# A scan kernel whose partitions hold four states by 32 channels in place of two states by 64

## The chip, the cores and the metric

The kernel runs on one core of one Trainium2 chip. The metric is the device time of one execution in microseconds, lower is better. The kernel before took 8292.5 us (median of 3 runs, 8291.23 to 8294.32). A core has four compute engines that run side by side, each with its own instruction queue: TensorE (PE) multiplies matrices, VectorE (DVE), ScalarE (ACT) and GpSimd (POOL) work elementwise, and SyncE (SP) issues the transfers. Data lies in SBUF, 128 partitions of plain memory, or in PSUM, eight banks that PE accumulates into. Transfers are moved by 16 DMA engines.

## The reference

The input is x of 8 x 512 x 48 x 48 in float32, so 8 samples of 512 channels and 2304 places. Layer 0 is a group norm and causal linear attention with a residual. Layer 1 is a group norm and then, for each of four blocks of 128 channels in turn, a Mamba block with 256 inner channels and 16 states. Its core is a recurrence in time, for every inner channel d and state n:

```
delta = softplus(dt @ Wdt.T + bdt);  A = -exp(A_log)
h[d,n] = exp(delta[d] * A[d,n]) * h[d,n] + (delta[d] * xs[d]) * B[n]      # one step in time
y[d]   = sum over n of h[d,n] * C[n]
y = (y + xs * D) * silu(z);  output = y @ Wo.T
```

B and C are 16 rows in time that all channels share; delta and dx = delta * xs are 256 rows in time that all states share.

## The kernel before

Time is cut into 6 chunks of LC = 384 places. A job is one chunk of one block of one sample; there are 8 x 4 x 6 = 192 jobs, taken from two streams in turn (even and odd samples). A job has 256 x 16 = 4096 recurrences, which fill 128 partitions 32 times, so it has 32 scans. They stand in 8 slots of 4 scans. In each slot the partitions hold 2 states (i) by 64 channels, and the four scans are two state pairs (j) by two groups of channels (g).

For each job the program prepares its operands (`prepare`, L697). ACT makes delta and POOL makes dx, both with 128 channels on the partitions. Two transfers write them to DRAM scratch (`spread`, L787), and others read them back in the layout of the scans: `dr` (delta, L802) and `dxr` (dx, L806), one tile for each half h of the 256 channels, each in two transfers of 64 partitions (`pairs`, L798). The rows of B and C go to DRAM scratch as well (`scr`, L763) and come back as four tiles each (`rows`, L810), a row being copied to 64 partitions by a source whose first dimension has step 0. All these transfers are issued by SP, in the order of the program.

A slot then works as follows.

- `decay` (L890): ACT writes exp(scale * dr) to a PSUM bank, once for each scan.
- `inputs` (L854): ACT copies the first 256 places of dxr to a PSUM bank as `dxp`, twice for each job.
- `product` (L881): DVE forms B * dx for the first 256 places, from B in SBUF and dxp in PSUM. `last_product` (L866): POOL forms the last 128 places, from SBUF.
- `scan` (L902): DVE runs the recurrence, 384 places for each scan.
- `weigh` (L915): POOL multiplies the four scans by C.
- `gather` (L930): PE adds the states of each channel into the bank `yp`, by a matrix of ones and zeros with 64 columns (`pair_sum`, L94), once for each scan.

Everything else (the convolution and gates of the Mamba block, the attention of later samples) is woven in between these slots. The order on every queue is written when the program is built: a slot is two halves, and a task says at which half its next step may be put (`yield first - 7, 0` means seven halves before its job's first slot; `Task`, L989, `beside`, L1069). In steady state a slot of job n carries the scans of job n, the preparation of job n + 1 and a piece of attention. `slot` (L1150) asks for `last_product` of slot k + 2 in the middle of slot k, and for `product` of slot k + 1 at the start of slot k.

Of the kernel before, what the change touches and what calls it, by code (L numbers as in the profile page):

```python
# [9 lines left out]
F32 = mybir.dt.float32  # L10
# [7 lines left out]
P = 128  # L18
T = 128
LC = 384  # L20
NG = 2
# [8 lines left out]
C_ID, C_MASK, C_GRP, C_ALL, C_TRI, C_SEL, C_END = 0, 128, 256, 384, 512, 640, 642  # L30


def constants():

    c = np.zeros((P, C_END), np.float32)
    p = np.arange(P)
    c[:, C_ID : C_ID + P] = p[:, None] == p[None, :]
    c[:, C_MASK : C_MASK + P] = p[:, None] <= p[None, :]
    c[:, C_GRP : C_GRP + P] = np.where(p[:, None] // 16 == p[None, :] // 16, 1.0 / 16.0, 0.0)
    same = p[:, None] % 64 == p[None, :] % 64  # L40
    c[:, C_ALL : C_ALL + P] = same
    c[:, C_TRI : C_TRI + P] = same & (p[:, None] // 64 <= p[None, :] // 64)

    for e in range(2):
        c[e * 64 : e * 64 + 64, C_SEL + e] = 1.0
    return c
# [3 lines left out]
def attention_then_mamba_kernel(  # L50
# [33 lines left out]
    k_all = cst[:, C_ALL : C_ALL + P]  # L84
# [8 lines left out]

    pair_sum = k_all[:, 0:64]  # L94
# [20 lines left out]
    w_a = scales[:, :, 596:628].rearrange("p s (h d) -> p s h d", h=4)  # L115
# [15 lines left out]
    drs = [cpool.tile([P, 2, 1 + LC], F32, name=f"dr_{i}") for i in range(2)]  # L131
# [392 lines left out]
    class Stream:  # L524
# [37 lines left out]
        def move_on(self):  # L562

            if self.b is not None and self.s < 3:
                self.s += 1
                self.fresh = False
            else:
                self.b, self.s = self.samples.pop(0), 0
                self.fresh = True
            self.ready = 0  # L570
            self.block += 1
            self.n = f"{self.b}_{self.s}"
            self.state = small.tile(
                [P, 2, NS // 2, 2], F32, tag=f"state{self.z}", name=f"state_{self.n}", bufs=1
            )
            self.fsum = small.tile([P, NC], F32, tag=f"fsum{self.z}", name=f"fsum_{self.n}", bufs=1)
            self.fm = dpool.tile([P, L], F32, tag="fm", name=f"fm_{self.n}")
            self.w = self.coming
# [111 lines left out]
    class Job:  # L690
# [6 lines left out]
        def prepare(self):  # L697
# [89 lines left out]
            def spread(what, of):  # L787
                to = dpool.tile([256, LC], F32, tag="dscr", name=f"{what}_{n}", bufs=6)
                nc.sync.dma_start(out=to.rearrange("(h p) l -> p h l", h=2), in_=of)
                return to.rearrange("(h g d) l -> h d g l", h=2, g=2)  # L790
# [5 lines left out]
            src = scr.rearrange("(q i m f) l -> q m i (f l)", q=4, m=2, i=2)  # L796

            def pairs(t, rows):  # L798
                for i in range(2):
                    nc.sync.dma_start(out=t[i * 64 : i * 64 + 64], in_=rows)  # L800

            def steps(h):  # L802
                self.dr[h] = drs[h]
                pairs(self.dr[h][:, :, 1 : 1 + LC], dsrc[h])

            def scaled(h):  # L806
                self.dxr[h] = mpool.tile([P, 2, LC], F32, tag="dxr", name=f"dxr_{n}_{h}")
                pairs(self.dxr[h], xsrc[h])

            def rows(m, q):  # L810
                t = mpool.tile([P, NG, LC], F32, tag="BC"[m], name=f"{'BC'[m]}_{n}_{q}", bufs=4)
                for i in range(2):
                    nc.sync.dma_start(
                        out=t[i * 64 : i * 64 + 64].rearrange("p j l -> p (j l)"),
                        in_=src[q, m, i].partition_broadcast(64),
                    )
                (self.B, self.C)[m][q] = t
# [7 lines left out]
            spreading.clear()  # L825
            yield first - 7, 0
            flush()
            steps(0)
            scaled(0)
            yield first - 6, 0  # L830
            rows(0, 0)
            yield first - 5, 0
            rows(0, 1)
            self.prepared = True
            yield first - 3, 0
            rows(0, 2)
            yield first - 2, 0
            rows(1, 0)
            yield first - 1, 0
            rows(0, 3)  # L840
            yield first, 0
            rows(1, 1)
            yield first + 1, 0
            scaled(1)
            yield first + 2, 0
            rows(1, 2)
            yield first + 3, 0
            steps(1)
            yield first + 4, 0
            rows(1, 3)  # L850
# [3 lines left out]
        def inputs(self, h):  # L854

            self.dxp = psx.tile([P, 2, LC - TAIL], F32, tag="dxp", name=f"dxp_{self.n}_{h}")
            nc.scalar.copy(self.dxp, self.dxr[h][:, :, 0 : LC - TAIL])  # L857
# [8 lines left out]
        def last_product(self, s):  # L866

            shape, cols = [P, NG, 2, TAIL], slice(LC - TAIL, LC)
            u = mpool.tile([P, NG, 2, 1 + LC], F32, tag="u", name=f"u_{self.n}_{s}", bufs=5)
            if self.c:  # L870
                h, q = s // 4, s % 4 * NG
                nc.scalar.copy(u[:, :, :, 0], self.state[:, h, q : q + NG, :])
            nc.gpsimd.tensor_tensor(  # L873
                u[:, :, :, 1 + LC - TAIL :],
                self.B[s % 4][:, :, cols].unsqueeze(2).to_broadcast(shape),
                self.dxr[s // 4][:, :, cols].unsqueeze(1).to_broadcast(shape),
                ALU.mult,
            )
            return u

        def product(self, s, u):  # L881

            shape, cols = [P, NG, 2, LC - TAIL], slice(0, LC - TAIL)
            nc.vector.tensor_mul(  # L884
                u[:, :, :, 1 : 1 + LC - TAIL],
                self.B[s % 4][:, :, cols].unsqueeze(2).to_broadcast(shape),
                self.dxp.unsqueeze(1).to_broadcast(shape),
            )

        def decay(self, s, i):  # L890
            h, q, j, g = s // 4, s % 4 * NG, i // 2, i % 2
# [6 lines left out]
                scale=w_a[:, self.w[1], 2 * h + g, q + j : q + j + 1],  # L898
# [3 lines left out]
        def scan(self, s, i, u, dA):  # L902
            j, g = i // 2, i % 2
            cols = slice(0 if self.c else 1, 1 + LC)
            nc.vector.tensor_tensor_scan(  # L905
                u[:, j, g, cols],
                dA[:, cols],
                u[:, j, g, cols],
# [6 lines left out]
        def weigh(self, s, u):  # L915

            nc.gpsimd.tensor_tensor(  # L917
                u[:, :, :, 0:LC],
                u[:, :, :, 1:],
                self.C[s % 4].unsqueeze(2).to_broadcast([P, NG, 2, LC]),  # L920
# [3 lines left out]
        def keep(self, s, u):  # L924

            h, q = s // 4, s % 4 * NG
            if self.c + 1 < NC:
                nc.scalar.copy(self.state[:, h, q : q + NG, :], u[:, :, :, LC])

        def gather(self, s, u):  # L930
            for j in range(NG):
                for g in range(2):
                    nc.tensor.matmul(  # L933
                        self.yp[g * 64 : g * 64 + 64, 0:LC],
                        pair_sum,
                        u[:, j, g, 0:LC],
                        start=False,
                        stop=(s % 4 == 3 and j == NG - 1),
                        skip_group_check=True,
                    )  # L940
# [209 lines left out]
    def slot(k):  # L1150
# [12 lines left out]
        for i in range(4):  # L1163
# [8 lines left out]
            if i == 1:  # L1172
# [5 lines left out]
                if s == 2:  # L1178
                    job.inputs(1)
# [125 lines left out]
```

## Time and profile before

The profiled execution took 8294.55 us by its own time, and its span, from the first to the last instruction, is 8292.4 us.

| engine | busy us | share of the span |
|---|---|---|
| DVE | 7952.3 | 96% |
| POOL | 7759.7 | 94% |
| PE | 7748.5 | 93% |
| ACT | 6911.0 | 83% |
| 16 DMA engines, mean of their packets' time | | 72% for SP's queue |

The first scan starts at 192.9 us and the last one ends at 8270.4 us. The 192 jobs therefore take 42.07 us each, a slot 5.26 us and a half 2.63 us. Busy time alone does not say what limits the kernel: one engine that is late in each job sets the pace of all, since every queue is served in order.

### The profile page before, as it was taken

The numbers are of one execution on the slowest core, as the hardware profiler recorded it, in microseconds if no ns is written. First come the engines' busy times: TensorE is split into PE (matmuls) and PEld (weight loads), VectorE is DVE, ScalarE is ACT, GpSimd is POOL, SyncE is SP. The second block draws the span as 40 slices with busy tenths as digits, with TensorE's granted clock in tenths as the row PEclk, the third lists the DMA queues.
The fourth block names the chain that finished last, engine by engine and source line by source line (L and its number), as shares of the span: only waits on it lengthen the run. The fifth ranks groups of instructions, "written<-read, shape, count | busy, mean of one in ns | idle before, by whom it ended". The sixth has DMA issues, their size and how long they took to land. (4 is left out here: it accounts for less than half of the span.)

```text
span 8292.4 us, 128570 instructions
## 1 busy us (share of the span) xinstructions
PE 7748.5 (93%) x38850; PEld 3744.1 (45%) x38850; DVE 7952.3 (96%) x10534; ACT 6911.0 (83%) x14630; POOL 7759.7 (94%) x4235
## 2 busy tenths in 40 slices
PE   8999999998999999999999999999999999999975
PEld 4444444444444444444444444444444444444432
DVE  3999999999999999999999999999999999999998
ACT  3888888887888888888888888888888888888876
POOL 2999999999999999999999999999999999999998
PEclk9999999999999999999999999999999999999987
DMA  6667777766777777777777777777777777777665
GB/s 202 190 190 204 210 206 209 208 193 197 208 204 201 201 208 209 204 205 196 201 207 201 197 205 209 208 208 193 202 200 207 201 201 197 201 200 196 191 169 145
DMA packets 974440, 1654.65 MB, mean 200 GB/s; under 512 B 119337, under 2 KB 768169, under 8 KB 973618
## 3 DMA queue, kind: packets, MB, share of 16 engines
q1 hardware_dynamic: 973746, 1646.43, 72.2%
q8 instruction: 309, 5.06, 0.3%
q14 instruction: 385, 3.15, 0.1%
HBM read 1318.28 MB, written 327.68 MB: 198 GB/s over the span
## 5 line engine op out<-in xcount | busy, mean ns | idle before, releaser
L905 DVE TENSOR_TENSOR_SCAN u<-bank,u 128x385 f32<-128x385 f32 (+1 forms) x6144 | 5439.5, 935 | 132.0 <-ACT bank L894 129.5
L917 POOL TENSOR_TENSOR u<-u,C 128x1536 f32<-128x1536 f32 x1536 | 4901.4, 3191 | 344.6 <-DVE u L905 147.3
L894 ACT ACTIVATE bank<-dr,scales 128x385 f32<-128x385 f32 (+1 forms) x6144 | 3411.6, 578 | 673.8 <-DVE u L905 639.4
L933 PE MATMUL yp<-u,cst 128*64 128x384 f32 x12288 | 2371.8, 507 | 236.2 <-ACT yp L862 160.3
L873 POOL TENSOR_TENSOR u<-B,dxr 128x512 f32<-128x512 f32 x1536 | 1977.2, 1287 | 17.3 <-DMA B<-scr 15.7
L884 DVE TENSOR_TENSOR u<-B,dxp 128x1024 f32<-128x1024 f32 x1536 | 1831.7, 1193 | 8.2 <-ACT dxp L857 8.2
L302 PE MATMUL bank<-xn,wq 128*128 128x384 f32 x4608 | 1659.1, 502 | 90.9 <-POOL xn L326 47.8
L933 PEld LDWEIGHTS yp<-u,cst 128*64 128x64 f32 x12288 | 776.5, 138 | 1412.3 <-issue 997.1
L302 PEld LDWEIGHTS bank<-xn,wq 128*128 128x128 f32 x4608 | 833.2, 191 | 838.4 <-DVE u L905 124.3
L709 PE MATMUL bank<-xi,wk 128*128 128x384 f32 x3072 | 1103.5, 502 | 9.5 <-POOL xi L683 6.3
L709 PEld LDWEIGHTS bank<-xi,wk 128*128 128x128 f32 x3072 | 556.2, 191 | 553.3 <-DVE u L905 94.0
L314 ACT ACTIVATE ex<-bank,bqkv_sb 128x384 f32<-128x384 f32 x384 | 220.3, 574 | 416.2 <-PE bank L302 416.1
L894 ACT ACT_TABLE_LOAD x382 | 490.1, 1283 | 6.7
L822 POOL TENSOR_TENSOR dx<-delta,xs 128x384 f32<-128x384 f32 x384 | 387.4, 1009 | 22.2 <-ACT delta L780 22.2
L951 PE MATMUL bank<-yz,scales 128*128 128x384 f32 x768 | 305.4, 514 | 38.4 <-DVE yz L945 30.6
L769 PE MATMUL bank<-dbc,steps_w 9*128 9x384 f32 x768 | 305.5, 517 | 3.4 <-ACT dbc L761 2.4
L720 PE MATMUL bank<-xi,scales 128*128 128x384 f32 x768 | 290.0, 492 | 2.6 <-ACT xs L745 2.1
L756 PE MATMUL bank<-xs,scales 128*40 128x384 f32 x768 | 279.5, 486 | 0.0
L857 ACT COPY dxp<-dxr 128x512 f32<-128x512 f32 x384 | 227.2, 592 | 37.0 <-DMA dxr<-xscr 19.2
L500 PE MATMUL bank<-sm,v 128*64 128x128 f32 x2304 | 253.0, 298 | 0.0
L745 ACT ACT_TABLE_LOAD x192 | 246.3, 1283 | 4.9 <-PE bank L709 1.5
L780 ACT ACT_TABLE_LOAD x192 | 246.3, 1283 | 4.0 <-issue 0.6
(118 smaller groups left out, 7907.2 us busy)
## 6 DMA issues: line engine op xcount, KB each, us to landing
B<-scr SPq DMA_DIRECT2D x1536, 192.0 KB, 4.6
C<-scr SPq DMA_DIRECT2D x1536, 192.0 KB, 5.2
xn<-xn SPq DMA_DIRECT2D x192, 768.0 KB, 7.1
dr<-dscr SPq DMA_DIRECT2D x768, 192.0 KB, 3.8
dxr<-xscr SPq DMA_DIRECT2D x768, 192.0 KB, 4.8
dscr<-delta SPq DMA_DIRECT2D x192, 384.0 KB, 6.9
xscr<-dx SPq DMA_DIRECT2D x192, 384.0 KB, 2.4
xn<-in_x SPq DMA_DIRECT2D x48, 768.0 KB, 6.6
```

The source lines that it names most:

```text
L302: nc.tensor.matmul(ps, wqs[m // NC][:, kt, j * P : (j + 1) * P], xn[:, kt, :], start=(kt == 0), stop=(kt == 3),)
L709: nc.tensor.matmul(xc, wk[:, k, h * P : (h + 1) * P], xi[:, c0 + k : c0 + k + LC], start=(k == 0), stop=(k == 3),)
L720: nc.tensor.matmul(zp, w_gate[:, s, h * P : (h + 1) * P], xi[:, c0 + 3 : c0 + 3 + LC], start=True, stop=True,)
L769: nc.tensor.matmul(vp, steps_w[32:41, s, h * P : (h + 1) * P], dbc[32:41, :], start=True, stop=True)
L822: nc.gpsimd.tensor_tensor(dx[:, h, :], delta[:, h, :], xs[:, h, :], ALU.mult)
L873: nc.gpsimd.tensor_tensor(u[:, :, :, 1 + LC - TAIL :], self.B[s % 4][:, :, cols].unsqueeze(2).to_broadcast(shape), self.dxr[s // 4][:, :, ...
L884: nc.vector.tensor_mul(u[:, :, :, 1 : 1 + LC - TAIL], self.B[s % 4][:, :, cols].unsqueeze(2).to_broadcast(shape), self.dxp.unsqueeze(1).to ...
L894: nc.scalar.activation(dA[:, cols], self.dr[h][:, g, cols], AF.Exp, scale=w_a[:, self.w[1], 2 * h + g, q + j : q + j + 1],)
L905: nc.vector.tensor_tensor_scan(u[:, j, g, cols], dA[:, cols], u[:, j, g, cols], 0.0, ALU.mult, ALU.add,)
L917: nc.gpsimd.tensor_tensor(u[:, :, :, 0:LC], u[:, :, :, 1:], self.C[s % 4].unsqueeze(2).to_broadcast([P, NG, 2, LC]), ALU.mult,)
L933: nc.tensor.matmul(self.yp[g * 64 : g * 64 + 64, 0:LC], pair_sum, u[:, j, g, 0:LC], start=False, stop=(s % 4 == 3 and j == NG - 1), skip_g ...
L951: nc.tensor.matmul(self.xm[:, 0:LC], w_out[:, self.w[1], h, :], self.yz[:, h, :], start=(h == 0), stop=(h == 1),)
```

## The change

The partitions hold 4 states (i) by 32 channels. In each slot the four scans are four groups of 32 channels (g) of one half, at one group of states (q). The states of a channel are now added by four products of 32 columns. A dxr or dr tile has four groups per partition where it had two, and B and C have two tiles per job where they had four. In `inputs`, B is copied to PSUM (`Bp`) and dxr is read from SBUF, with four copies for each job. The transfers change in form, number and order:

```
             def spread(what, of):
                 to = dpool.tile([256, LC], F32, tag="dscr", ...)
-                nc.sync.dma_start(out=to.rearrange("(h p) l -> p h l", h=2), in_=of)
-                return to.rearrange("(h g d) l -> h d g l", h=2, g=2)
+                for h in range(2):
+                    nc.sync.dma_start(
+                        out=to.rearrange("(h c g) l -> h g c l", h=2, g=NGR)[h],
+                        in_=of[:, h, :],
+                    )
+                return to.rearrange("(h c g) l -> h c g l", h=2, g=NGR)
             def steps(h):
-                pairs(self.dr[h][:, :, 1 : 1 + LC], dsrc[h])
+                for i in range(NI):
+                    nc.sync.dma_start(
+                        out=self.dr[h][i * 32 : i * 32 + 32, :, 1 : 1 + LC], in_=dsrc[h]
+                    )
             def scaled(h):
-                self.dxr[h] = mpool.tile([P, 2, LC], F32, tag="dxr", ...)
-                pairs(self.dxr[h], xsrc[h])
+                self.dxr[h] = mpool.tile([P, NGR, LC], F32, tag="dxr", ...)
+                rows = xsrc[h].rearrange("c g l -> c (g l)")
+                nc.sync.dma_start(
+                    out=self.dxr[h].rearrange("p g l -> p (g l)"),
+                    in_=rows.unsqueeze(0).to_broadcast([NI, 32, NGR * LC]),
+                )
-            def rows(m, q):
-                t = mpool.tile([P, NG, LC], F32, tag="BC"[m], ..., bufs=4)
-                for i in range(2):
-                    nc.sync.dma_start(
-                        out=t[i * 64 : i * 64 + 64].rearrange("p j l -> p (j l)"),
-                        in_=src[q, m, i].partition_broadcast(64),
-                    )
+            def rows(m, half):
+                t = mpool.tile([P, 2, LC], F32, tag="BC"[m], ..., bufs=2)
+                src = scr.rearrange("(m q i f) l -> m q i (f l)", m=2, q=2, i=NI)[m, half]
+                nc.sync.dma_start(
+                    out=t.rearrange("p f l -> p (f l)"),
+                    in_=src.unsqueeze(1).to_broadcast([NI, 32, 2 * LC]),
+                )
```

The transfers stand at these halves relative to the job's first slot. Before: dr 0 and dxr 0 at -7, B at -6, -5, -3, -1, C at -2, 0, 2, 4, dxr 1 at 1, dr 1 at 3. After: B 0 at -8, dr 0 and dxr 0 at -7, B 1 at -4, C 0 at -2, dxr 1 at 0, dr 1 at 1, C 1 at 3.

```
-        def inputs(self, h):
-            self.dxp = psx.tile([P, 2, LC - TAIL], F32, tag="dxp", ...)
-            nc.scalar.copy(self.dxp, self.dxr[h][:, :, 0 : LC - TAIL])
+        def inputs(self, pair):
+            self.Bp = psx.tile([P, 2, LC - TAIL], F32, tag="Bp", ...)
+            nc.scalar.copy(self.Bp, self.B[pair % 2][:, :, 0 : LC - TAIL])
         def product(self, s, u):
-                self.B[s % 4][:, :, cols].unsqueeze(2).to_broadcast(shape),
-                self.dxp.unsqueeze(1).to_broadcast(shape),
+                self.Bp[:, s % 2, :].unsqueeze(1).to_broadcast(shape),
+                self.dxr[s // NQ][:, :, cols],
         def gather(self, s, u):
-            for j in range(NG):
-                for g in range(2):
-                    nc.tensor.matmul(self.yp[g * 64 : g * 64 + 64, 0:LC], pair_sum, u[:, j, g, 0:LC], ...)
+            for g in range(NGR):
+                nc.tensor.matmul(self.yp[g * 32 : g * 32 + 32, 0:LC], state_sum, u[:, g, 0:LC], ...)
         # in slot(), in the middle of a slot
-                if s == 2:
-                    job.inputs(1)
+                if s in (0, 2, 4):
+                    job.inputs(s // 2 + 1)
```

`decay`, `scan`, `weigh`, `keep` and `last_product` change their indices alone: the same number of instructions on as many elements. The order of instructions on PE, DVE and POOL stays as it was.

## The prediction

> **What bounds the kernel now.** I read the page's busy shares first, then the groups by line, then the waits, then the transfers.
>
> ```profile
> PE 7748.5 (93%) x38850; PEld 3744.1 (45%) x38850; DVE 7952.3 (96%) x10534; ACT 6911.0 (83%) x14630; POOL 7759.7 (94%) x4235
> ...
> DMA packets 974440, 1654.65 MB, mean 200 GB/s; under 512 B 119337, under 2 KB 768169, under 8 KB 973618
> ...
> q1 hardware_dynamic: 973746, 1646.43, 72.2%
> ...
> L905 DVE TENSOR_TENSOR_SCAN u<-bank,u 128x385 f32<-128x385 f32 (+1 forms) x6144 | 5439.5, 935 | 132.0 <-ACT bank L894 129.5
> L917 POOL TENSOR_TENSOR u<-u,C 128x1536 f32<-128x1536 f32 x1536 | 4901.4, 3191 | 344.6 <-DVE u L905 147.3
> ...
> L884 DVE TENSOR_TENSOR u<-B,dxp 128x1024 f32<-128x1024 f32 x1536 | 1831.7, 1193 | 8.2 <-ACT dxp L857 8.2
> ...
> L857 ACT COPY dxp<-dxr 128x512 f32<-128x512 f32 x384 | 227.2, 592 | 37.0 <-DMA dxr<-xscr 19.2
> ```
>
> DVE bounds it: 7952 of 8292 us, of which some 150 lie before the first scan, so it is nearly gapless in the 192 jobs. Scans and products are 7271 us of that. Transfers hardly show: on DVE the longest wait is for ACT's decays (129.5 us). But SP's queue keeps the 16 DMA engines 72% busy on average, so they have a reserve of 1.4 times, and only if the load is spread evenly.
>
> The list of transfers, by line, with KB each and median us from issue to landing:
>
> ```profile
> B<-scr SPq DMA_DIRECT2D x1536, 192.0 KB, 4.6
> C<-scr SPq DMA_DIRECT2D x1536, 192.0 KB, 5.2
> ...
> dr<-dscr SPq DMA_DIRECT2D x768, 192.0 KB, 3.8
> dxr<-xscr SPq DMA_DIRECT2D x768, 192.0 KB, 4.8
> dscr<-delta SPq DMA_DIRECT2D x192, 384.0 KB, 6.9
> xscr<-dx SPq DMA_DIRECT2D x192, 384.0 KB, 2.4
> ...
> steps_w<-in_wdt SPq DMA_DIRECT2D x1, 36.0 KB
> ```
>
> **What the skill says.** (1) The Trainium skill, "DMA: Bandwidth & Descriptors", section "Why a DMA increments its semaphore by 16 and not by 1": a transfer issued by SP runs on k engines, k being the largest number up to 16 that divides the slowest dimension (other than 1) of both access patterns; they are the lowest-numbered k, and each posts one completion. (2) Its "Rules for kernel authors": a leading broadcast of c copies confines the transfer to at most c engines. The trace agrees where it can be tested. The list's counts add up to 7451 transfers; 16 completions each would be 119,216 packets of 4 bytes, and with the 128 rows of 48 bytes of bqkv (its 6 KB) 119,344 packets under 512 B. The page has 119,337, which is 7 fewer: the one transfer with 9 rows, steps_w, posted 9. It is also the one without a landing time. No transfer of before with a first dimension of 4 exists. (3) "SBUF — State Buffer", "Door 1: The DMA port swizzle": partitions p and p + 32 share a port. Packet records agree for reads: isolated ksum stores, 64 partitions, took 115 ns for 1536 bytes in the median, xscr stores on 128 partitions 66 ns. (4) Same page, "Who interferes with whom": DVE with one SBUF input does not contend with GpSimd; product has one SBUF and one PSUM input both ways.
>
> **The change part by part.**
>
> *DVE, POOL, PE:* as many instructions on as many elements, in the same order. Product swaps which input is in PSUM; I keep 1193 ns (bounds: 3% either way on 1832 us, 55 us). POOL's rows keep 1287 and 3191 ns. Gather keeps its 12,288 matmuls at 507 ns, with loads of 32 columns where 64 took 138 ns; PE weight loads overlap. Constants and memsets differ before the first scan by under 1 us.
>
> *ACT:* four copies per job for two. 384 x 592 ns = 227 us more. ACT has 1381 us idle, 639.4 of them waiting for DVE to free a decay's bank; that covers it. Without cover it is 227 us. Behind a late copy wait the decays, and behind them DVE's scans.
>
> *SP:* per job two spreads become four, 8 reads of dr and dxr become 10, 16 of B and C become 4: 18 issues for 26, near 0.6 us each in the timeline, 5 us less. SP is not on the path; worth nothing by itself.
>
> *Bytes:* the same. B and C halve from 604 to 302 MB (3072 x 196,608 bytes before), dr and dxr double from 302 to 604, spreads stay at 151.
>
> *Where the bytes go* is the step that decides. As the instructions carry them, B and C have a source of 4 rows x 32 copies (step 0) on a target of 128 partitions; dxr has 4 copies (step 0) x 32 rows on 128; a spread has a target of 4 x 32 rows from 128. By (1) all run on k = 4 engines, the same four. Only dr (32 on both sides) keeps 16. Per job and engine of the four:
>
> - dxr: 2 x 786,432 bytes / 4 = 393 KB
> - B and C: 4 x 393,216 / 4 = 393 KB
> - spreads: 4 x 196,608 / 4 = 197 KB
> - dr: 8 x 196,608 / 16 = 98 KB
> - everything else: 1646.4 - 604 - 302 - 151 = 589.4 MB, / 192 jobs / 16 = 192 KB
>
> Sum 1273 KB, where it was 1646.43 MB / 192 / 16 = 536 KB. The page's rate of an engine while busy is 1646.43 MB / (0.722 x 16 x 8292.4 us) = 17.2 KB/us. So the four need 1273 / 17.2 = 74.1 us per job, against the job's 42.07 us. They become the bound, and the other twelve idle.
>
> *Sum:* head 192.9 + 192 x 74.1 + tail 22.0 (8292.4 - 8270.4) = 14,440 us, against a span of 8292.4 (own time 8294.55; the median 8292.5 is the same to 0.03%).
>
> *Bounds on the rate.* Fast: the best packets in the records are 65 ns for 1536 bytes, 119 for 3072, 234 for 6144. Then dxr 64 x 234 = 15.0, B and C 128 x 119 = 15.2, spreads 128 x 65 = 8.3, dr 64 x 65 = 4.2, others about 115 x 65 = 7.5, and 1.1 for larger packets and completions: 51.3 us, or 10,065 us in all. Slow: engines 0 and 1 walk partitions 0-31 and 32-63 together, and by (3) share a port at each step, as 2 and 3 do. At the ksum ratio (115/65) on dxr, B, C and spreads: 38.5 x 1.77 + 12.8 = 80.9 us, or 15,760; with rates fully halved, 89.8 us and 17,460. I take the mean rate of before, since its B rows also came in 64-partition transfers and its 3072-byte packets took 191 ns in the mean.
>
> *What is late next.* dxr 0 is issued at half -7 and needed by last_product at half -3, 10.5 us later; 197 KB per engine at 17.2 KB/us take 11.4 us alone, behind B 0's 5.7 and xscr's 5.7. So POOL waits there, with weigh queued behind it; then DVE's product (now a direct reader of dxr), its scans, and the PSUM banks that ACT's decays need. dxr 1 (half 0 to 5) and C 1 (half 3 to 6, 7.9 us) are late too. Every transfer on all 16 engines queues behind the same four, so attention's xr, xn and before arrive late and stall PE.
>
> **The rivals.**
>
> *A. Four engines, but at nearly their best packet rate* (51 to 62 us per job): 10,065 to 12,100, some 10,500 with idle gaps. For it: twelve engines are nearly silent, and half of the 1536-byte packets already take 65 ns. Against: the shared port.
>
> *B. Four engines with ports fully shared:* 15,800 to 17,500, more if the chain xscr, dxr, last_product leaves the engines empty between. For it: the ksum packets. Against: two engines drift apart.
>
> *C, on the other side: the transfers run on 16 engines after all,* because the splitter follows the 128 partitions on the SBUF side. For it: only one transfer of before had fewer than 16, and its 9 rows stood on both sides. Then the load per engine stays 536 KB, with larger dxr packets and 8 issues fewer per job. It frees POOL's 48.2 us before weigh and ACT's 19.2 us of waits for transfers, less what the ACT copies add: about 8270 us, between 8200 and 8340. It decides at k: with k = 8 the load is 755 MB / 192 / 8 + 290 = 782 KB, or 45.5 us, already over 42.07; so only k = 16 escapes.
>
> *D. No engine limit, but the four copies make decays late:* uncovered 227 us, 8520. Against: ACT's 639 us of slack. It goes with C's slow edge.
>
> **How the numbers follow.** The forecast case, 12,000 to 15,800: 0.56. A, below 12,000: 0.18. B above 15,800: 0.09. C with D: 0.17, of which 0.07 faster, 0.05 within 0.2% (about what a measurement of this kernel can tell from no change) and 0.05 slower. Faster 0.07, same 0.05, slower 0.88. The forecast is 14,440. The range from 9,800 to 17,000 holds the first two cases and most of B; C and B's end are left out, some 0.2. The forecast case's own range is 12,000 to 15,800.
>
> **What would show it.** Right: the page's mean DMA share falls to some 40% ((4 x 100% + 12 x 23%) / 16) while time rises; GB/s falls to about 115; packets under 512 B fall to about 71,720, since ten transfers per job post 4 completions (2459 other transfers x 16 - 7 + 192 x (8 x 16 + 10 x 4) + 128), where 16 engines for all would leave 94,760; landing times of dxr and B rise past 10 us; POOL, ACT and DVE wait for DMA dxr, B and C, and DVE's share falls to about 55%. The rows for scans, products and weigh keep 935, 1193 and 3191 ns. Wrong: landings of dxr near 5 us, a DMA share near 70% and a DVE share of 95% would mean that the transfers were spread, and the whole sum falls.

## The result, and the profile after

The kernel after took 11,127.55 us (median of 4 runs, 11,116.35 to 11,155.28) against 8293.41 us for the kernel before (4 runs beside them, 8291.23 to 8298.3): a ratio of 1.342, with a 95% interval of 1.340 to 1.344. The profiled execution took 11,132.0 us, its span 11,130.2.

The forecast was 14,440 us. The direction and the mechanism stand, and the time lies in the wide range from 9,800 to 17,000, but the loss is 2834 us where 6147 were forecast, and the forecast case's own range, 12,000 to 15,800, is missed. This is rival A, four engines at nearly their best packet rate, to which the prediction gave 0.18.

Three words are used below. A packet is one piece that a DMA engine moves, here mostly of 1536, 3072 or 6144 bytes. A completion is the packet of 4 bytes that each engine of a transfer posts at its end. A narrow transfer is one that posts fewer than 16 completions.

The page of the kernel after, with the lines that answer to those shown of before: busy times, transfers, the chain that ended last, and the groups (busy us, mean ns of one, idle time just before them and what ended it):

```profile
PE 8279.8 (74%) x38850; PEld 3844.8 (35%) x38850; DVE 8026.9 (72%) x10534; ACT 7141.4 (64%) x15014; POOL 7764.6 (70%) x4235
...
DMA packets 877653, 1654.25 MB, mean 149 GB/s; under 512 B 71721, under 2 KB 720553, under 8 KB 876850
...
q1 hardware_dynamic: 876978, 1646.19, 49.5%
...
DMA 68%; PE 8%; DVE 8%; POOL 6%; issue 4%; ACT 3%; SPq 2%; POOLq 0%; ACTq 0%; DVEq 0%
...
L900 DVE TENSOR_TENSOR_SCAN u<-bank,u 128x385 f32<-128x385 f32 (+1 forms) x6144 | 5447.1, 938 | 504.1 <-ACT bank L890 423.3
L913 POOL TENSOR_TENSOR u<-u,C 128x1536 f32<-128x1536 f32 x1536 | 4882.7, 3179 | 1129.2 <-DMA C<-scr 740.9
...
L869 POOL TENSOR_TENSOR u<-B,dxr 128x512 f32<-128x512 f32 x1536 | 1958.6, 1275 | 1964.1 <-DMA dxr<-xscr 1502.7
L880 DVE TENSOR_TENSOR u<-Bp,dxr 128x1024 f32<-128x1024 f32 x1536 | 1849.7, 1204 | 1611.2 <-DMA dxr<-xscr 1589.5
...
L853 ACT COPY Bp<-B 128x512 f32<-128x512 f32 x768 | 447.7, 583 | 404.6 <-DMA B<-scr 366.4
...
dxr<-xscr SPq DMA_DIRECT2D x384, 768.0 KB
```

DVE is busy for 75 us more than before and the span is 2838 us longer: the loss is waiting, not work. The scan (935, now 938 ns), the product (1193, 1204) and weigh (3191, 3179) are what they were. DVE waited 8.2 us ahead of its product before and waits 1611.2 now, nearly all for dxr; POOL waited 17.3 us ahead of `last_product` and waits 1964.1; the line of before is

```profile
L873 POOL TENSOR_TENSOR u<-B,dxr 128x512 f32<-128x512 f32 x1536 | 1977.2, 1287 | 17.3 <-DMA B<-scr 15.7
```

The same bytes (1646 MB) keep the 16 engines busy for 49.5% in place of 72.2%, yet transfers make up 68% of the chain that ended last. That is the picture of a few full engines beside many idle ones. The packets under 512 B are 71,721, where the prediction had 71,720 for ten transfers per job on four engines and 94,760 for all on 16.

Of the waits of the kernel after (us in total, times, longest us):

```profile
ACT bank L890 <- DVE u L900: 1695.3, 847, 9.6
DVE u L880 <- DMA dxr<-xscr: 1589.5, 274, 10.9
POOL u L869 <- DMA dxr<-xscr: 1502.7, 265, 26.1
...
PE bank L484 <- DMA xr<-in_x: 355.5, 149, 6.8
```

The first is the echo of the others: ACT has no free bank because DVE, which frees them, stands still. The last is attention's `xr`, a transfer on all 16 engines that comes late behind the narrow ones, as predicted.

The first scan ends the head at 201.2 us, and the 192 jobs take 11,104.7 + 0.9 - 201.2 = 10,904.4 us, so 56.8 us each (before 42.07). The four engines carry 1273 KB in that time: 22.4 KB/us, where the prediction took 17.2.

### The profile page after: what moved, and what is told of

Its sections match the earlier page's. It is cut to its first block, busy times and chain, and to the rows that moved or that the text cites. A ratio compares the mean times of both kernels' runs of the same rounds, so it can differ in the third digit from the quotient of the medians.

```text
span 11130.2 us, 126063 instructions
## 1 busy us (share of the span) xinstructions
PE 8279.8 (74%) x38850; PEld 3844.8 (35%) x38850; DVE 8026.9 (72%) x10534; ACT 7141.4 (64%) x15014; POOL 7764.6 (70%) x4235
## 2 busy tenths in 40 slices
DMA packets 877653, 1654.25 MB, mean 149 GB/s; under 512 B 71721, under 2 KB 720553, under 8 KB 876850
## 3 DMA queue, kind: packets, MB, share of 16 engines
q1 hardware_dynamic: 876978, 1646.19, 49.5%
## 4 chain that ended last, share of the span: by engine, by line
DMA 68%; PE 8%; DVE 8%; POOL 6%; issue 4%; ACT 3%; SPq 2%; POOLq 0%; ACTq 0%; DVEq 0%
DMA dxr<-xscr 25%; DMA C<-scr 21%; DMA xscr<-dx 8%; DVE u L900 5%; DMA dr<-dscr 4%; DMA fu<-fm 3%; POOL u L913 3%; DMA xn<-xn 2%; DMA B<-scr 2%; PE bank L300 2%; DVE u L880 1%; POOL u L869 1%; ACT bank L890 1%; PE bank L754 1%; DMA xs<-in_x 1%
## 5 line engine op out<-in xcount | busy, mean ns | idle before, releaser
L913 POOL TENSOR_TENSOR u<-u,C 128x1536 f32<-128x1536 f32 x1536 | 4882.7, 3179 | 1129.2 <-DMA C<-scr 740.9
L869 POOL TENSOR_TENSOR u<-B,dxr 128x512 f32<-128x512 f32 x1536 | 1958.6, 1275 | 1964.1 <-DMA dxr<-xscr 1502.7
L880 DVE TENSOR_TENSOR u<-Bp,dxr 128x1024 f32<-128x1024 f32 x1536 | 1849.7, 1204 | 1611.2 <-DMA dxr<-xscr 1589.5
L927 PE MATMUL yp<-u,cst 128*32 128x384 f32 x12288 | 1576.2, 590 | 676.4 <-ACT yp L858 320.9
L300 PE MATMUL bank<-xn,wq 128*128 128x384 f32 x4608 | 1924.4, 568 | 113.4 <-DVE k L367 95.8
L300 PEld LDWEIGHTS bank<-xn,wq 128*128 128x128 f32 x4608 | 982.1, 225 | 1004.6 <-issue 265.4
L754 PE MATMUL bank<-xs,scales 128*40 128x384 f32 x768 | 520.3, 831 | 1031.0 <-DVE u L900 1031.0
L927 PEld LDWEIGHTS yp<-u,cst 128*32 128x32 f32 x12288 | 268.7, 116 | 1407.0 <-issue 493.0
L853 ACT COPY Bp<-B 128x512 f32<-128x512 f32 x768 | 447.7, 583 | 404.6 <-DMA B<-scr 366.4
L939 DVE TENSOR_TENSOR yz<-yp,sz 128x384 f32<-128x384 f32 x384 | 211.9, 552 | 530.6 <-PE yp L927 530.6
L484 PE MATMUL bank<-xr,cst 128*128 128x384 f32 x384 | 229.0, 687 | 413.6 <-DMA xr<-in_x 355.5
L767 PE MATMUL bank<-dbc,steps_w 9*128 9x384 f32 x768 | 416.8, 675 | 9.0 <-ACT dbc L759 4.1
```

The lines of the kernel that those rows point to most:

```text
L300: nc.tensor.matmul(ps, wqs[m // NC][:, kt, j * P : (j + 1) * P], xn[:, kt, :], start=(kt == 0), stop=(kt == 3),)
L754: nc.tensor.matmul(dps[0:40, 0:LC], w_x[:, s, h, :], xs[:, h, :], start=(h == 0), stop=(h == 1))
L767: nc.tensor.matmul(vp, steps_w[32:41, s, h * P : (h + 1) * P], dbc[32:41, :], start=True, stop=True)
L853: nc.scalar.copy(self.Bp, self.B[pair % 2][:, :, 0 : LC - TAIL])
L869: nc.gpsimd.tensor_tensor(u[:, :, 1 + LC - TAIL :], self.B[q // 2][:, q % 2, cols].unsqueeze(1).to_broadcast(shape), self.dxr[h][:, :, col ...
L880: nc.vector.tensor_mul(u[:, :, 1 : 1 + LC - TAIL], self.Bp[:, s % 2, :].unsqueeze(1).to_broadcast(shape), self.dxr[s // NQ][:, :, cols],)
```

## The experiments

Three theories were held against each other. Theory 1: the bytes of all narrow transfers pile up on the same four engines, and these set the pace. Theory 2: the new layout itself costs the time (copies on ACT, dxr read from SBUF by DVE, four products). Theory 3: it is not the load but the flight time of a narrow transfer against its lead. "Per job" below is the span less 224 us for head and tail (226 in the kernel after), divided by 192. A time without a range is that of a single run; the four of the kernel after lie within 0.35% of each other.

**Every narrow transfer cut so that both its sides start with 32.** The layout, the copies and the bytes stay.

```
-                in_=rows.unsqueeze(0).to_broadcast([NI, 32, NGR * LC])      # dxr, one transfer of 128 partitions
+            for i in range(NI):
+                out=self.dxr[h][i * 32 : i * 32 + 32], in_=rows               # four of 32
-                in_=src.unsqueeze(1).to_broadcast([NI, 32, 2 * LC])           # B, C
+            for i in range(NI):
+                out=t[i * 32 : i * 32 + 32], in_=src[i].partition_broadcast(32)
-                out=to...[h], in_=of[:, h, :]                                 # spreads
+                for g in range(NGR): out=to...[h, g], in_=of[g * 32 : g * 32 + 32, h, :]
```

> The changed layout as it is, with every transfer of the change cut so that both sides begin with a dimension of 32: dxr, B and C in four transfers of 32 partitions each, each spread in four of 32 rows. Same bytes, same packet sizes, 48 issues per job in place of 18. Theory 1 (four engines carry 1273 KB per job each, at the 22.4 KB/us that the changed kernel shows): the load per engine falls to 536 KB, the DMA engines no longer bind, and the job returns to DVE's pace, 42 to 43.5 us, 8,300 to 8,560 us in all; packets under 512 B rise to about 163,900 (2459 x 16 - 7 + 192 x 48 x 16 + 128 = 186,921 if each posts 16). Theory 2 (the layout itself costs: twice the dxr and dr bytes, dxr read by DVE, four ACT copies, fewer buffers): it stays near 11,100 us.

Measured: 8336.69 us (8331.15 to 8339.67), a ratio to before of 1.0052 (1.0036 to 1.0069). The page:

```profile
PE 7195.6 (86%) x38850; PEld 3397.4 (41%) x38850; DVE 7964.2 (96%) x10534; ACT 7079.5 (85%) x15014; POOL 7759.9 (93%) x4235
...
DMA packets 992918, 1655.25 MB, mean 199 GB/s; under 512 B 186921, under 2 KB 835753, under 8 KB 992050
...
q1 hardware_dynamic: 992178, 1646.65, 75.1%
```

98% of the loss is gone, with 48 issues per job where the kernel after has 18. Theory 2 falls: without the narrow transfers 44 us of the loss are left. The packets under 512 B are what 16 completions for each transfer make: 39,337 for the other 2459 transfers, 147,456 for 48 x 192 and 128 for bqkv give 186,921. (The smaller number in the expectation was a slip of the sum.)

**The same confinement put into the kernel before.** Only its B and C are changed: each pair of transfers of 64 partitions becomes one with a first dimension of 2.

```
-                for i in range(2):
-                    out=t[i * 64 : i * 64 + 64], in_=src[q, m, i].partition_broadcast(64)
+                out=t, in_=src[q, m].unsqueeze(1).to_broadcast([2, 64, NG * LC])
```

> The kernel before, in its own layout, with one edit: each pair of transfers for a B or C tile becomes one, from a source of 2 rows x 64 copies. Half the issues for the same bytes. Theory 1: these run on 2 engines, which then carry 3146 KB / 2 + (8575 - 3146) / 16 = 1912 KB per job; at 22.4 KB/us that is 85 us per job, about 16,600 us. Packets under 512 B fall to 119,337 - 1536 x 30 = 73,257. Theory 2 (layout): no loss, about 8,290 us or slightly less for the fewer issues.

Measured: 15,751.5 us. The page, its transfers and two groups:

```profile
DMA packets 928340, 1654.29 MB, mean 105 GB/s; under 512 B 73258, under 2 KB 722090, under 8 KB 927539
...
q1 hardware_dynamic: 927666, 1646.25, 32.4%
...
L916 POOL TENSOR_TENSOR u<-u,C 128x1536 f32<-128x1536 f32 x1536 | 4873.0, 3173 | 4914.7 <-DMA C<-scr 4194.1
...
L883 DVE TENSOR_TENSOR u<-B,dxp 128x1024 f32<-128x1024 f32 x1536 | 1860.0, 1211 | 4552.1 <-DMA B<-scr 3861.3
```

The same bytes, in eight issues per job fewer, take nearly twice the time, in the old layout. The two engines carry 604 MB / 192 / 2 = 1573 KB of B and C and 1042.4 MB / 192 / 16 = 339 KB of the rest; at 80.9 us per job that is 23.6 KB/us. These two have work throughout: between 1000 and 7000 us fewer than two packets are in flight for 1.4% of the time, exactly two for 63%.

**dxr on two engines in place of four**, all else as in the kernel after.

```
-            in_=rows.unsqueeze(0).to_broadcast([NI, 32, NGR * LC])
+            for i in range(2):
+                out=self.dxr[h][i * 64 : i * 64 + 64], in_=rows.unsqueeze(0).to_broadcast([2, 32, NGR * LC])
```

> The changed kernel with each dxr transfer cut in two, each from 2 copies x 32 rows, so on 2 engines by theory 1. Engines 0 and 1 then carry dxr 1573 / 2 = 786 KB, B and C 393, spreads 197, the rest 290: 1666 KB per job; at 22.4 KB/us 74.4 us, about 14,500 us. If the engines of a narrow transfer were not always the lowest-numbered ones, the load would spread over four and the time stay near 11,100 us.

Measured: 14,026.78 us, 71.9 us per job. Its waits:

```profile
POOL u L870 <- DMA dxr<-xscr: 3435.2, 260, 34.1
DVE u L881 <- DMA dxr<-xscr: 3326.6, 248, 23.3
```

The two fullest engines now carry 786 + 393 + 197 + 98 + 192 = 1666 KB, at 23.2 KB/us. Both waits for dxr have more than doubled. Fewer than two packets are in flight for 0.2% of the time.

**Load that no operand depends on.** The kernel with all transfers cut (8337 us) gets four more transfers per job, 768 KB each, from 4 copies of 32 rows, so on four engines; they write DRAM that nothing reads.

```
+            def junk():
+                t = dpool.tile([P, NGR * LC + 64], F32, tag="junk", ..., bufs=16)
+                out=t[:, 0 : NGR * LC], in_=xsrc[0]....unsqueeze(0).to_broadcast([NI, 32, NGR * LC])
+            junk()        # at four places of a job's preparation
```

> e1_all16 plus four extra transfers per job of 768 KB each, from dx's scratch with a leading dimension of 4 copies to a scratch in DRAM that nothing reads. They add 786 KB to each of the four engines, so that these carry 1322 KB per job. Theory 1 (the load of the fullest engines sets the pace, in order, whoever waits for what): 128 packets of 6144 bytes at 253 ns are 32.4 us, with 536 KB at 22.4 KB/us, 23.9 us, together 56 us per job, about 11,000 us, although no instruction waits for the added transfers. Theory 3 (the loss comes from the longer flight of each dxr, B and C transfer against the lead that the timetable gives it): these are as short as in e1_all16, so the time is that of e1_all16.

Measured: 12,687.18 us, 64.9 us per job. Its queue, and the longest of SP's waits (us in total, times, longest us):

```profile
q1 hardware_dynamic: 1093554, 2250.65, 60.5%
...
SPq L822 <- DMA junk<-xscr: 2035.2, 306, 7.7
```

No operand of the kernel comes over a narrow transfer here, and it still loses 4350 us. Theory 3 as it was stated, by which the time would have been that of the cut kernel, falls. But the added transfers are not quite without anyone who waits for them: no compute engine does, yet SP, which issues all transfers in order, waits 4665 us in all for their landings (why it waits is told below). So the run shows what load on four engines costs when no operand is part of it. It does not tell how much of the cost is operands that queue behind this load on the engines and how much is operands that SP issues late. The four engines have work nearly throughout: fewer than four packets are in flight for 5.6% of the time.

The expectation, 56 us per job, was too low because it moved the 536 KB of the cut kernel at 22.4 KB/us, the rate of four engines at work with few others. At the cut kernel's own pace they take 75.1% of 42.3 us = 31.8 us; with 128 packets of 6144 bytes at 253 ns = 32.4 the sum is 64.2.

**One kind of transfer spread at a time**, by the same edits as in the first experiment: dxr alone, B and C alone, the spreads alone.

> The kernel after with dxr alone spread over 16 engines (four transfers of 32 partitions for each half); B, C and the spreads stay on four. Theory 1 (the bytes of all transfers on the four shared engines set the pace): the four keep 1273 - 393 + 98 = 978 KB per job. By the packet times of the runs so far, 128 packets of B and C at 154 ns = 19.7, 16 of dxr at 403 ns (as with 16 engines on 32 partitions) = 6.4 and 307 of 1536 bytes at 65 to 89 ns = 19.9 to 27.3: 46.0 to 53.4 us per job, 9,030 to 10,460 us. Theory 3 (what counts is the flight time of dxr, the transfer that POOL and DVE wait for longest, against its lead): with dxr at its lead again nearly all is recovered, about 8,400 to 8,600.

> The kernel after with B and C alone spread over 16 engines; dxr and the spreads stay on four. Theory 1: the same 978 KB per job on the four as with dxr spread: 64 packets of dxr at 270 ns = 17.3, 32 of B and C at 185 ns = 5.9, 307 of 1536 bytes at 65 to 89 ns = 19.9 to 27.3: 43.1 to 50.5 us per job, 8,480 to 9,900 us, and so no more than with dxr spread. Theory 3: dxr flies as long as before the cut, and only the waits for B and C go (366 us on ACT and 741 us on POOL of the kernel after): about 10,000 to 10,400 us, far more than with dxr spread.

> The kernel after with the spreads (dscr, xscr) alone on 16 engines; dxr, B and C stay on four. Theory 1: 1273 - 197 + 49 = 1125 KB per job on the four: dxr 17.3, B and C 19.7, 211 packets of 1536 bytes at 65 to 89 ns = 13.7 to 18.8: 50.7 to 55.8 us per job, 9,930 to 10,920 us. Theory 3: the spread is one link of the chain xscr, dxr; with it shorter by some 5 us of a job, about 10,100. This run does not tell the two apart; it prices the third part, so that the three parts can be added up.

Measured: 9804.23, 10,285.1 and 11,851.34 us. Of the 2791 us that all three together win back, dxr alone brings 1323, B and C alone 842, and the spreads alone cost 724. They do not add up, and neither theory foresaw all three. The time with dxr cut lies in theory 1's range and far above theory 3's; that with B and C cut lies in theory 3's range (10,000 to 10,400) and above theory 1's (8,480 to 9,900); that with the spreads cut lies above both. With equal loads (978 KB), B and C should have won at least as much as dxr by theory 1. Load alone is thus not the whole account of a partial repair. Two things are seen in the traces.

First, packets beside cut transfers take longer. The 6144-byte packets of dxr took 270 ns in the mean in the kernel after and 357 with B and C cut; the 3072-byte packets of B and C took 154, and 186 with dxr cut, 171 with the spreads cut. With dxr cut, the four engines have work as steadily as in the kernel after (the table below), so there the slower packets are what keeps the rate at 19.6 KB/us.

Second, SP itself is held. In the traces SP's transfers signal their landing on eight semaphores (flags on which engines wait) in turn, and in the kernel after 5537 of the 5915 first wait on the semaphore that they are about to use, so for the landing of the transfer eight places ahead. The longest waits of SP's queue (us in total, times, longest us), first before, then after, then with the spreads cut:

```profile
SPq L789 <- POOL dx L822: 1085.2, 192, 9.1
SPq L178 <- ACT bank L894: 611.0, 182, 6.9
```

```profile
SPq L801 <- DMA C<-scr: 634.4, 149, 5.1
SPq L353 <- DMA dxr<-xscr: 457.7, 94, 9.3
```

```profile
SPq L789 <- DMA C<-scr: 635.5, 192, 5.8
SPq L802 <- DMA C<-scr: 629.6, 149, 5.3
```

Before, SP waits for work of the engines; after, it waits for landings, and a spread (L789 of the cut kernel) that needs nothing of C waits for C. More and smaller transfers would make this window of eight reach less far ahead, and the four engines run dry more often. Packets in flight are counted from the packet records between 1000 and 7000 us, the waits over the whole span:

| kernel | KB per job on the fullest engines | us per job | KB/us | under 4 packets in flight | SP's waits for landings, us |
|---|---|---|---|---|---|
| before | 536 | 42.07 | (hidden) | 23% | 312 |
| after | 1273 | 56.8 | 22.4 | 0.9% | 3041 |
| dxr cut | 978 | 49.9 | 19.6 | 1.1% | 4018 |
| B, C cut | 978 | 52.4 | 18.7 | 4.3% | 4138 |
| spreads cut | 1125 | 60.6 | 18.6 | 8.0% | 4163 |
| spreads cut, 8 issues fewer (below) | 1125 | 58.1 | 19.4 | 6.0% | 3802 |
| dxr on two engines | 1666 | 71.9 | 23.2 | (under 2: 0.2%) | 2888 |
| before, B, C on two engines | 1912 | 80.9 | 23.6 | (under 2: 1.4%) | 1440 |
| all cut | 536 | 42.2 | (hidden) | 16% | 601 |
| all cut, load added | 1322 | 64.9 | 20.4 | 5.6% | 5957 |

**The spreads cut into fewer transfers.** Same engines, same packets, 22 issues per job in place of 30.

```
-                for h in range(2):
-                    for g in range(NGR):
-                        out=to.rearrange("(h c g) l -> h g c l", ...)[h, g], in_=of[g * 32 : g * 32 + 32, h, :]
+                for g in range(NGR):
+                    out=to.rearrange("(h c g) l -> g c h l", ...)[g], in_=of[g * 32 : g * 32 + 32]
```

> The kernel with the spreads alone on 16 engines (11,851 us, slower than the kernel after), with each spread in four transfers of 32 partitions and both halves in place of eight of one half: 22 issues per job in place of 30, the same packets on the same engines. In that kernel fewer than 4 packets are in flight for 8% of the time (under 1% in the kernel after), 4.9 us per job, and SP waits 4163 us for transfers to land (before 313, after 3041). If the loss comes from SP, whose every transfer waits for the landing of the one eight places ahead of it, so that more and smaller transfers reach less far ahead, the empty time shrinks: 10,950 to 11,350 us, with SP's waits for transfers below 3,600 us. If it comes from slower packets (32 partitions on 16 engines beside the four), nothing changes: 11,700 to 11,900 us.

Measured: 11,390.12 us, just above the first expectation and well below the second. Of the 724 us that cutting the spreads cost, eight issues fewer brought 461 back. The packets are no faster (3072 bytes at 171 ns, 6144 at 282 in both), so the gain is not theirs. The empty time fell from 8.0% to 6.0%, which by the us per job is some 260 us in all, and SP's waits from 4163 to 3802 us, where below 3600 was expected. So the window is part of the price of cutting; where the other 200 us of the gain came from was not settled. Nor was it how the 263 us that remain against the kernel after divide between slower packets and the four issues more.

**The other order of the partitions.** In place of cutting, channel and state change places: partition = channel * 4 + state. Then every source of dr, dxr, B and C starts with 32 and every target has 128 partitions, with few transfers (22 per job; the spreads go back to one each, and the weights' order follows).

```
-    c[:, C_SUM : C_SUM + 32] = p[:, None] % 32 == p[None, :32]
+    c[:, C_SUM : C_SUM + 32] = p[:, None] // 4 == p[None, :32]
-                in_=rows.unsqueeze(0).to_broadcast([NI, 32, NGR * LC])                          # dxr, once
+                in_=xsrc[h][:, g, :].unsqueeze(1).to_broadcast([32, NI, LC])                     # for each g; dr alike
-                in_=src.unsqueeze(1).to_broadcast([NI, 32, 2 * LC])                             # B, C
+                in_=src.unsqueeze(0).to_broadcast([32, NI, 2 * LC])
```

> The kernel after with the partition order turned round: partition = channel * 4 + state in place of state * 32 + channel, so that every source and target of dr, dxr, B and C starts with 32, and 16 engines share each transfer with no cut along the partitions; the spreads have the old form, one each. dr and dxr go in four transfers each (one for each group, 1536 bytes in a packet), B and C in one each: 22 issues per job, where the kernel with every narrow transfer cut in four had 48. Theory 1 (engines alone): 1646 MB / 192 / 16 = 536 KB per engine and job again, hidden: 8,290 to 8,350 us. If the cut transfers of 32 partitions, whose 6144-byte packets took 403 ns, or the 48 issues made the 44 us that the cut kernel lost against before, this one is at before, 8,285 to 8,300; if it is the layout itself (768 ACT copies, dxr read by more), it stays at 8,320 to 8,345.

Measured: 8315.89 us (8311.15 to 8319.82), a ratio of 1.0026 (1.0017 to 1.0035). Its queue, and the landing of dxr:

```profile
q1 hardware_dynamic: 1059762, 1646.33, 60.6%
...
dxr<-xscr SPq DMA_DIRECT2D x1536, 192.0 KB, 3.9
```

For the same bytes the engines are busy 60.6% where the cut kernel had 75.1%, and SP's waits for landings are 38 us. About half of the cut kernel's 44 us thus went with the cutting, and 21 us stay with the layout.

**Is it the copies on ACT?** The kernel before with two more copies of dxp per job, and the kernel just shown with three copies of B per job in place of four (the second half takes states 8 to 15 first; the two buffers of B and C, which the program gave out freely, take fixed turns for it).

```
+                if s in (0, 4):                                            # before, in the middle of a slot
+                    nc.scalar.copy(job.dxp, job.dxr[s // 4][:, :, 0 : LC - TAIL])
```

> The kernel before with two more copies of dxp per job on ACT (slots 0 and 4; they write the same values again), 384 x 592 ns = 227 us more ACT work, all else as before. If the extra copies of the four-state layout make the 44 us that the kernel with all transfers cut lost against before, this kernel loses the same: 8,325 to 8,350 us, with DVE's waits for ACT's decays up from 129.5 us by about 40. If ACT's idle time covers them as the prediction held, it stays within 8,276 to 8,309, and the 44 us come from the transfers.

```
-            h, q = s // NQ, s % NQ
+            h = s // NQ; q = (s + 2 * h) % NQ
-                if s in (0, 2, 4):
-                    job.inputs(s // 2 + 1)
+                if s in (0, 4):
+                    job.inputs(1 + s // 4)
```

> The kernel with the four states interleaved (partition = channel * 4 + state, 8315.9 us) with the second half's slots taking the two tiles of B in the opposite order (states 8 to 15 first), so that the copy of B to PSUM between the halves falls away: three copies per job on ACT in place of four, 192 x 587 ns = 113 us less. Nothing else changes. By the 51 us that 384 more copies cost in the kernel before, it gains half of that, 25 us: 8,290. If ACT's copies are hidden in this layout, it stays at 8,311 to 8,320. At 8,275 or less it would beat the kernel before.

Measured: 8345.55 us with two more copies (ratio 1.0061, 1.0046 to 1.0076), 8318.63 us with one fewer (8314.19 to 8320.2). Two of DVE's waits with two more copies:

```profile
DVE u L905 <- ACT bank L894: 158.4, 173, 5.0
DVE k L369 <- ACT bank L315: 57.4, 66, 3.9
```

384 more copies of 579 ns, 222 us of ACT, cost the kernel before 51 us, of which 47 are these two waits (129.5 and 39.3 before). Yet taking 113 us away in the new layout gains nothing: the wait for decays is 113.6 us with four copies and 111.8 with three. So the copies have a price where they are put in without need, and the last 21 us of the new layout were not shown to be theirs. By its trace the interleaved kernel is busy on DVE for 7 us more than before, and DVE's wait for ACT ahead of attention's q grew from 38.0 to 72.6 us while that for decays fell from 129.5 to 113.6. Three things differ that could be behind it: the third copy, the granted TensorE clock (0.93 in the kernels with four products of 32 columns and hidden transfers, 0.98 before), and attention's products (574 ns for 502), for which ACT waited 378 times in place of 241, though for 414 us in all as before (416). That stays open.

**The kernel before with its partitions interleaved** (channel * 2 + state): 18 transfers per job for 26, B and C in one transfer each.

```
-                for i in range(2):
-                    out=t[i * 64 : i * 64 + 64], in_=src[q, m, i].partition_broadcast(64)
+                out=t, in_=src[q, m].unsqueeze(0).to_broadcast([64, 2, NG * LC])
```

> The kernel before with its partition order turned round: partition = channel * 2 + state in place of state * 64 + channel. B and C come in one transfer of 128 partitions each in place of two of 64, dr and dxr in two by group of channels: 18 issues per job for 26, all on 16 engines. Nothing else changes. If the issues or the 64-partition transfers of before cost anything, it is faster: POOL's 48 us of waits before weigh and ACT's 19 us for dxr are what there is to win, so 8,240 to 8,295; with no gain within 0.2%, 8,276 to 8,309. If packets to interleaved partitions are slower, DVE would wait for B or ACT, above 8,310.

Measured: 8290.13 us (8283.18 to 8293.64), a ratio of 0.9994 (0.9985 to 1.0002): no difference that can be measured.

```profile
q1 hardware_dynamic: 949170, 1646.33, 59.9%
```

The engines' share fell from 72.2% to 59.9%, and nothing came of it: with DVE busy for 96%, the transfers of before were hidden. No version that was run is measurably faster than the kernel before.

## Why the prediction was right in kind and wrong in size

- *Which transfers are confined, and to how many engines:* right. 71,720 small packets were predicted and 71,721 counted; merging B and C of the kernel before gave 73,258 where 73,257 were expected. The Trainium skill, "DMA: Bandwidth & Descriptors", section "Why a DMA increments its semaphore by 16 and not by 1", thus agrees for k = 2, 4 and 16.
- *That they share the same four engines, 1273 KB per job, and that this load becomes the bound:* right. Fewer than four packets are in flight for only 0.9% of the time. Spreading all of them returns 98% of the loss, two engines in place of four make it larger at nearly the same KB/us, and load of no use on four engines makes a loss of its own.
- *The rate, 17.2 KB/us, and with it 1273 / 17.2 = 74.1 us per job:* this step failed. The four engines moved 22.4 KB/us, 56.8 us per job. The 17.2 are the mean of the kernel before, whose transfers of B, C, dr and dxr reach 64 partitions at a time, on 16 engines, with 12 or more packets in flight for nearly all of these. In the kernel after dxr, B and C reach 128 partitions, and four engines run alone for about half of the time (exactly four packets in flight for 49%). The mean ns of a packet, by the number of packets in flight at its start, with the kernel before interleaved in the last column:

| bytes | after, 1 to 6 | after, 12 and more | before, 1 to 6 | before, 12 and more | before interleaved, 12 and more |
|---|---|---|---|---|---|
| 1536 | 72.6 | 89.2 | 85 | 84 | 73 |
| 3072 | 133.9 | 177.8 | 206 | 191 | 146 |
| 6144 | 252.7 | 328.0 | | 264 | 278 |

  With the means of its first column the sum would have been 64 x 252.7 = 16.2 us for dxr, 128 x 133.9 = 17.1 for B and C and 307 x 72.6 = 22.3 for the rest: 55.6 us per job. The measured 56.8 lie inside rival A's 51 to 62. The prediction had the numbers for it, in the best packets of before (65, 119, 234 ns); it took the busy mean, although its own argument emptied twelve of the engines. But how many packets are in flight is not the whole reason: in the kernel before, packets are no faster with few in flight, and in the kernel before interleaved they are faster with many, where 16 engines move 1646.33 MB / (0.599 x 16 x 8290.5 us) = 20.7 KB/us each while busy. So the mean of before was low in good part by the form of its transfers, which the new ones do not share. How much of the 22.4 is the new form and how much the quiet of the other twelve engines was not settled.
- *The shared port as a reason against A:* did not show at four engines. A 6144-byte packet took 238 ns in the median, as the best of before (234), so the slow bound, which let the engines meet on a port at each step, had no ground here; no trace shows which partitions an engine walks. Such packets were slow where 16 engines write the same 32 partitions: 424 ns in the cut kernel. The Trainium skill, "SBUF — State Buffer", section "Door 1: The DMA port swizzle", by which 32 partitions in a row reach half of the ports, fits this second case; that the port is the cause was argued, not measured apart. Rival B falls. (80.9 us per job make 15,748 us, not the 15,760 of the sum; nothing hangs on it.)
- *Compute rows:* right within 1% for scan, product and weigh. The gather took 590 ns, not 507: see the last section.
- *SP is not on the path:* true of issue times, but SP's window of eight was overlooked. It does not bound the kernel after, whose four engines have work throughout; it is part of what a partial repair costs.
- *ACT's idle time covers the copies:* right in the new layout for the one copy that was taken away, wrong as a rule: two copies more cost the kernel before 51 us.
- *The signs of it:* share, GB/s and DVE's share moved as said (40%, 115, 55% forecast; 49.5%, 149, 72% measured), each off by about the factor by which the time was, 1.3 (1.24 for the share). Landings of dxr past 10 us could not be read, since the page gives none for transfers without 16 completions; the longest wait for dxr, 26.1 us, stands in for it.
- *Rival C* (16 engines after all, about 8270 us) fell with the packet count. *Rival D* (the copies alone, 8520 us) can be read with the transfers on 16 engines: 8316 and 8337 us, 21 and 44 above before, where 227 were its price.

## What to carry to other kernels

Before a tensor is laid out anew, write down the first dimension of both sides of every transfer, and add up per iteration what lands on the few engines that all narrow transfers share; a broadcast with few copies on the outside can make a kernel slower by a third at equal bytes, and putting the channel outside and the few states inside avoided it here with 22 transfers per job, where cutting took 48. When a change alters the form of transfers, or leaves most engines idle, do not price them at the busy mean of the old ones: packets of the same size took from 134 to 206 ns here. Repair such a fault whole, and measure a partial repair before keeping it: of three parts here two gained 1323 and 842 us and one cost 724, since the packets beside cut transfers were slower and more transfers filled the queue's window.

## What was not expected of the hardware

- Two full engines moved 23.2 and 23.6 KB/us each, four 22.4, and 16 together, while busy, 17.2 before, 16.4 with all transfers cut, 20.4 and 20.7 with partitions interleaved (four states, two states).
- Products into four column groups of 32 overlap more than those into two of 64: 12,288 of them, 513 ns each, keep PE busy for 1354.9 us in the interleaved kernel, where 507 ns each made 2371.8 us before (ends of matmuls are modelled in the profile, so how much they overlap is rough). PE fell from 93% to 86% of the span, which gained nothing, as DVE sets the pace.
- The granted TensorE clock went down with the share of the span for which PE is busy: 0.983 at 93% (before), 0.93 at 86% (all transfers cut, or interleaved), 0.807 at 74% (after), 0.75 at 61 to 66% (two engines, or load added). The gather's products were longer at the lower clock (590 ns after, 515 with all transfers cut). Which brings about the other was not tried; PE makes up 8% of the chain that ended last in the kernel after.
